# Attention in pairs of key blocks: full units of row maxima, VectorE's order written out, division two steps late, clearing spread out

## The chip, the cores and the metric

The kernel runs on one core of one Trainium2 chip. The metric is the device time of one execution in microseconds (us); lower is better. The engines are named as in the profile: PE (TensorE, matmuls), PEld (its weight loads), DVE (VectorE), ACT (ScalarE), POOL (GpSimd) and SP (SyncE, which here only issues DMAs).

## The reference, cut to what matters

The input x is 2 x 1024 tokens of 512 numbers, in float32. Four residual layers follow one another, each on the layer-normed x: causal attention with 16 heads of 32, a mixture of 32 experts of which each token takes the 8 with the largest router logits, a state-space layer (in chunks of 64), and a gated feed-forward whose weights are looked up in a table of 16 numbers. The change lies in the attention and in the routing that is interleaved with it:

```python
x = x + attn(_layernorm(x))
x = x + experts(_layernorm(x))      # router: top 8 of 32, softmax over them
x = x + ssd(_layernorm(x))
x = x + ghost_ffn(_layernorm(x))

def attn(x):
    q = einsum('btc,hcd->bhtd', x, Wq) + bq     # k, v likewise
    scores = einsum('bhtd,bhsd->bhts', q, k) * scale
    probs = softmax(scores + causal)
    y = einsum('bhts,bhsd->bhtd', probs, v)
    return y.reshape(B, T, H * D) @ Wo + bo
```

## The kernel before, in words

Attention (`_attention`) works on groups of four heads of one batch: four groups per batch, so eight groups, 0 to 7. The 1024 tokens of a batch are eight blocks of 128. A group's queries come as two halves (qt 0 and 1) of 512; with the causal mask the first half sees key blocks 0 to 3 and the second 0 to 7, so a group has twelve steps (qt, kb), and `group` (L660) loops over them.

The softmax is made in two passes. The row maxima come first and from a matmul of their own. `maxima` (L432) computes, for each query block tb and each pair pr of heads, the scores of that block against its keys in pieces of at most 512 keys, two heads (hh) at a time in two PSUM tiles `sp`; VectorE reduces them into `mx`: `junk` (L462) masks and reduces the diagonal 128 keys, and a `tensor_reduce` (L468) the rest. A piece of one (tb, pr) is one unit, so there are 8 x 2 units for the first 512 keys and 4 x 2 for the others: 24 steps of the generator's loop per group, many of them with fewer than four blocks of keys. `fold` (L473) turns the maxima of half a group, negated, with a transposing matmul (`nm_ps`) and ACT copies (L487) them into extra rows of q, so that the second pass subtracts them within its matmul.

The second pass has `scores` (L524) and `values` (L554). `scores` makes four matmuls `st` (one per head) for one step; ACT takes their exp into `pT` (L544), and POOL clears the triangle of a diagonal block (L547). `values` multiplies `pT` with v, where 32 columns of ones beside the values make the row sums, into two PSUM tiles `y`. After the last key block of a half, `finish` (L496) divides: ACT copies `y` to `raw`, four DMAs write the sums to DRAM, one DMA reads them back spread over 128 partitions (`sm`), VectorE takes the reciprocal (L509), one DMA writes it (`inv`), four DMAs broadcast it (`rb`), and four multiplications on VectorE give `yT` (L519). `finish` stands, whole, at the place where the half ends.

The groups are pipelined: while group i runs its twelve steps, `maxima(i + 1)` is interleaved, and at its end `project_qk(i + 2)` (L401: four `pq` of four matmuls; VectorE adds the bias for q, L423, ACT for k, L427), with the last `values` after the first `pq`. Beside a group something else may run, one generator step at a time: `normalise(1)` (layer norm of the second batch, from group 1 on) and `route_first` (L585: routing of the first batch's eight blocks in four pairs, and after each pair its 16 sends, in groups 4 on). Group 4 also holds `project_v` of the second batch. `project_out(0)` stands between groups 3 and 4, and `route_last` with `project_out(1)` after group 7.

A send (`_Router.send`, L253) is an indirect DMA on POOL that writes 128 token rows to their slots in `rows`, in DRAM. The slots must have been cleared: `clear` (L334) has 178 DMAs on SP's queue, 160 of 272.5 KB into `rows` and 18 of 256 KB into the accumulators. Four are issued at each step of a group, without a wait on anything of the group, and SP's queue is the one that the DMAs of `finish`, the weights and the routing use too. The sends wait for the clears of `rows` (the list `ready`). The routed rows (`row`, written at L162) lie in a pool of three buffers, of which `blank`, the source of the clears, holds one; the rows of a later pair take a buffer again only when the sends that read it are done.

PSUM has eight banks: two of tag "f" (maxima, projections, nm_ps, routing), four of tag "s" (`st`) and two for `y`. PE's order is the program's order, because the attention is built inside `manual_schedule(engines={PE})`; the order of VectorE, ACT, POOL and SP is left to the scheduler. Whatever an engine's instruction waits for, what is queued behind it on that engine waits too.

Of the kernel before, what the change touches and what calls it, by code (L numbers as in the profile page):

```python
# [18 lines left out]
P = 128  # L19
# [82 lines left out]
class _Router:  # L102
# [7 lines left out]
    def __init__(self, tc, g, x_sb, xnT, a, pool, rows, acc, left, ready):  # L110
        nc = tc.nc
        self.tc, self.g, self.x_sb, self.xnT = tc, g, x_sb, xnT
        self.pool, self.rows, self.acc, self.left, self.ready = pool, rows, acc, left, ready
        self.sent = [[[] for _ in range(TOPK)] for _ in range(B)]
        self.earlier = None
        self.over = pool.tile([P, 1], I32, tag="over", name="over")
        self.wr = pool.tile([P, NCC, E], F32, tag="wr", name="wr")
        nc.scalar.dma_start(out=self.wr, in_=a["wr"])
        self.ones = pool.tile([P, P], F32, tag="ones", name="ones")
        nc.gpsimd.memset(self.ones, 1.0)  # L120
        self.before = pool.tile([P, P], F32, tag="before", name="before")
        nc.gpsimd.affine_select(
            self.before, self.ones, pattern=[[1, P]], compare_op=ALU.is_gt, fill=0.0, base=0,
            channel_multiplier=-1,
        )
        self.number = pool.tile([P, NBLK], I32, tag="number", name="number")
        nc.gpsimd.iota(self.number, pattern=[[P, NBLK]], base=0, channel_multiplier=1)
        self.spare = pool.tile([P, NBLK, TOPK], I32, tag="spare", name="spare")
        nc.gpsimd.iota(
            self.spare, pattern=[[P * TOPK, NBLK], [P, TOPK]], base=1 + E * CAP,  # L130
            channel_multiplier=1,
        )
        self.first = pool.tile([P, E], I32, tag="first", name="first")
        nc.gpsimd.iota(self.first, pattern=[[CAP, E]], base=1, channel_multiplier=0)
# [10 lines left out]
    def route(self, blocks, wk, row_of, bank):  # L145

        tc, g, x_sb, xnT = self.tc, self.g, self.x_sb, self.xnT
# [20 lines left out]
        for i, blk in enumerate(blocks):  # L168
            pt = bank("t", [P, NCC, P])
            for cc in range(NCC):  # L170
                nc.tensor.transpose(
                    pt[:, cc, :], xr[i][:, cc * P : (cc + 1) * P], g["ident"]
                )
            nc.scalar.copy(xnT[:, :, blk * P : (blk + 1) * P], pt)
            yield
        pl = bank("l", [P, n, E])
        for i, blk in enumerate(blocks):
            for cc in range(NCC):
                nc.tensor.matmul(
                    pl[:, i, :], lhsT=xnT[:, cc, blk * P : (blk + 1) * P],  # L180
                    rhs=self.wr[:, cc, :], start=cc == 0, stop=cc == NCC - 1,
                )
# [65 lines left out]
    def send(self, routed, places):  # L248
        tc = self.tc
        blocks, xr, idx = routed  # L250
        for k in places:
# [12 lines left out]
            yield  # L264
# [16 lines left out]
def _attention(tc, g, x_sb, xnT, a, router):  # L281
# [8 lines left out]
    with ExitStack() as ctx:  # L290
# [6 lines left out]
        rp = inner.enter_context(tc.tile_pool(name="at_row", bufs=3))  # L297
# [36 lines left out]
        def clear():  # L334
            for n in range(E * CAPB):
                ready.append(
                    nc.sync.dma_start(out=rows[1 + n * P : 1 + (n + 1) * P, :], in_=blank)
                )
                yield
            for n in range(NBLK + 1):  # L340
                nc.sync.dma_start(out=acc[1][n * P : (n + 1) * P, :], in_=blank[:, :D])
                yield
            nc.sync.dma_start(out=acc[0][NT : NT + P, :], in_=blank[:, :D])
            yield

        clearing = clear()


# [3 lines left out]

        v = kv.tile([P, TBLK, H // 2, 3, DH], F32, tag="v", name="v")
# [9 lines left out]
        def normalise(b):  # L363

            for grp in range(TBLK // 4):
# [4 lines left out]
                for i, blk in enumerate(blocks):  # L370
# [3 lines left out]
                    before = xn, blk  # L374
# [7 lines left out]
        def project_v(b):  # L382
            for sb in range(TBLK):
                pv = ps_f.tile([P, D], F32, tag="f", name="pv")
                for cc in range(NCC):
                    nc.tensor.matmul(
                        pv,
                        lhsT=xnT[:, cc, b * T + sb * P : b * T + (sb + 1) * P],
# [12 lines left out]
        def project_qk(i):  # L401
# [4 lines left out]
            for hf in range(2):  # L406
                tok = slice(hf * 512, (hf + 1) * 512)
                for s, (dst, wn) in enumerate(((q, "wq"), (k, "wk"))):
                    pq = ps_f.tile([P, 512], F32, tag="f", name="pq")
                    for cc in range(NCC):  # L410
# [3 lines left out]
                            rhs=xnT[:, cc, b * T + hf * 512 : b * T + (hf + 1) * 512],  # L414
# [16 lines left out]

        def maxima(i, psum, tag):  # L432
# [3 lines left out]
                [P, TBLK, 2, 2, 3], F32, tag="mx", name="mx", bufs=2  # L436
            )
            nc.gpsimd.memset(mx, F32_MIN)
            for tb in range(TBLK):
                n = (tb + 1) * P  # L440
                for pr in range(2):
                    for ci, k0 in enumerate(range(0, n, 512)):
                        k1 = min(n, k0 + 512)
                        sp = [
                            psum.tile([P, 512], F32, tag=tag, name="sp") for _ in range(2)
                        ]
                        for hh in range(2):
                            rows = slice(hh * 64, hh * 64 + 64)
                            nc.tensor.matmul(  # L449
                                sp[hh][:, : k1 - k0],  # L450
                                lhsT=q[rows, pr, tb * P : (tb + 1) * P],
                                rhs=k[rows, pr, k0:k1],
                                start=True,
                                stop=True,
                            )
                        for hh in range(2):
                            m = mx[:, tb, pr, hh]
                            rest = k1 - k0
                            if k1 == n:
                                rest -= P  # L460
                                junk = wk.tile([P, P], F32, tag="junk", name="junk", bufs=1)
                                nc.vector.tensor_tensor_reduce(  # L462
                                    out=junk, in0=sp[hh][:, rest : rest + P], in1=cmask,
                                    scale=1.0, scalar=F32_MIN, op0=ALU.add, op1=ALU.max,
                                    accum_out=m[:, 2:3],
                                )
                            if rest:
                                nc.vector.tensor_reduce(  # L468
                                    m[:, ci : ci + 1], sp[hh][:, :rest], AX.X, ALU.max
                                )  # L470
                        yield
# [23 lines left out]

        def finish(i, qt, y):  # L496

# [10 lines left out]
            nc.sync.dma_start(out=sm, in_=sums.rearrange("j (c f) -> (j c) f", f=16))  # L508
            nc.vector.reciprocal(sm, sm)  # L509
            nc.sync.dma_start(out=inv.rearrange("j (c f) -> (j c) f", f=16), in_=sm)  # L510
            rb = wk.tile([P, 2, 512], F32, tag="rb", name="rb", bufs=1)
            for j in range(4):
# [3 lines left out]
                )  # L516
            for j in range(4):
# [6 lines left out]
        def scores(i, qt, kb):  # L524
# [5 lines left out]
            for j in range(4):  # L530
# [9 lines left out]
                pT = router.pool.tile(  # L540
                    [P, ROW], F32, tag=f"row{turn[0] % TBLK}", name="pT"
                )[:, :512]
                turn[0] += 1
                nc.scalar.activation(pT[:, c0:], st[:, c0:], AF.Exp)  # L544
# [7 lines left out]
            return ps  # L552

        def values(i, qt, kb, ps, y):  # L554
# [11 lines left out]
            if kb == 4 * qt + 3:  # L566
                finish(i, qt, y)
# [17 lines left out]
        def route_first():  # L585

            def bank(tag, shape):
# [5 lines left out]
            for blk in range(0, TBLK, 2):  # L593
                routed = yield from router.route([blk, blk + 1], wk, row_of, bank)
                yield from router.send(routed, range(TOPK))
# [43 lines left out]
        def first_groups():  # L639
# [12 lines left out]
            for u, _ in enumerate(maxima(0, ps_s, "s")):  # L652
                if u % 2:
                    next(other)
                if u == 11:
# [4 lines left out]
        def group(i, beside):  # L660
# [7 lines left out]
            pending = y = None  # L668
            blocks = [(qt, kb) for qt in range(2) for kb in range(4 * qt + 4)]
            for n, (qt, kb) in enumerate(blocks):  # L670
                if kb == 0:
                    y = [ps_y.tile([P, 512], F32, tag="y", name="y") for _ in range(2)]
                ps = scores(i, qt, kb)
                next(more, None)
                for _ in range(4):
                    next(clearing, None)
                next(beside, None)
                if n == 1 and gi == 0 and b:
                    run(project_v(b))
                    load_w("wo", "wvo")  # L680
                if pending is not None:
                    values(*pending)
                pending = (i, qt, kb, ps, y)
                next(more, None)
                next(beside, None)
                if n == 5 and follows:
                    fold(i + 1, 0)
            ahead = project_qk(i + 2) if i + 2 < ngr else iter(())
            next(ahead, None)
            values(*pending)  # L690
            run(ahead)
            if follows:
# [3 lines left out]
        with tc.manual_schedule(engines={mybir.EngineType.PE}):  # L696
            first_groups()
            fold(0, 1)
            beside = iter(())
            for i in range(ngr):  # L700
                if i == 1:
                    beside = normalise(1)
                group(i, beside)
                if i == NG - 1:
                    run(beside)
                    run(project_out(0, yT[0]))
                    load_w("wv", "wvo")
                    beside = route_first()
            run(beside)
        y = yT[0]  # L710
# [224 lines left out]
def _left_over(tc, g, x_sb, xnT, a, left, acc):  # L935
# [3 lines left out]
    with ExitStack() as ctx:  # L939
# [5 lines left out]
        dr = ctx.enter_context(tc.tile_pool(name="ex_dr", bufs=1, space=DRAM))  # L945

        wT = dr.tile([E, NT], F32, tag="wT", name="wT")
# [465 lines left out]
def kernel(ctx: ExitStack, tc: tile.TileContext, a: dict, out: bass.AP):  # L1413
# [26 lines left out]
    with tc.tile_pool(name="tokens", bufs=1, side="right") as tok:  # L1440
        x_sb = tok.tile([P, NBLK, D], F32, tag="x", name="x_sb")
        xnT = tok.tile([P, NCC, NT], F32, tag="xnT", name="xnT")
        router = _Router(tc, g, x_sb, xnT, a, pool, rows, acc, left, [])
        _attention(tc, g, x_sb, xnT, a, router)
# [4 lines left out]
        with tc.If(some > 0):  # L1449
            _left_over(tc, g, x_sb, xnT, a, left, acc[0])  # L1450
# [130 lines left out]
```

## Time and profile before

| what | us |
| --- | --- |
| median of three runs | 3076.01 (3062.91 to 3078.62) |
| the profiled execution | 3071.58 |
| its span on the profile | 3069.7 |
| PE busy, of the span | 2794.5 (91%) |
| DVE busy | 1381.8 (45%) |
| ACT busy | 915.5 (30%) |
| POOL busy | 617.9 (20%) |
| mean clock granted to PE | 0.951 |
| norms, first projections, maxima of group 0 (12.8 to 104.3) | 91.5 |
| the eight groups with project_out(0) (104.8 to 852.5) | 747.7 |
| after attention, up to the experts' first matmul (to 976.5) | 124.0 |
| experts and the second layer (to the end) | 2093.2 |

The profile is of one execution. Busy time is the time in which an engine executes something; [...] The granted clock is 1.00 at full speed. A row of waits reads "engine, what it waited to do, what it waited for: us in total, times, longest". A row of a timeline reads "start, duration, engine, line, operation, how many in one stretch", and in brackets the idle time before it and what ended that.

### The profile page before, as it was taken

Reading aid. Unit: us, or ns where it says so; the run is one execution under the profiler, and the core shown is the slowest. Engines: PE = TensorE matmul, PEld = TensorE weight load, DVE = VectorE, ACT = ScalarE, POOL = GpSimd, SP = SyncE. Lnnn points to the kernel's source line nnn. Section 1 sums busy time; section 2 is a strip of 40 time slices with the busy share of each in tenths; the row PEclk is TensorE's granted clock in tenths of the full one; section 3 lists DMA queues with packets and bytes.
Section 4 is the critical chain, followed back from the end, with each engine's and each line's share of the span. In section 5 each row is a group of like instructions: output and inputs, shape, how many; then the busy total and the mean of one; then the engine's idle time right before and its main releaser. Section 6 shows DMA issues by size and latency. Waiting matters only on the chain. (4 is left out here: it accounts for less than half of the span.)

```text
span 3069.7 us, 34003 instructions
## 1 busy us (share of the span) xinstructions
PE 2794.5 (91%) x11848; PEld 1612.2 (53%) x11848; DVE 1381.8 (45%) x3803; ACT 915.5 (30%) x1863; POOL 617.9 (20%) x786
## 2 busy tenths in 40 slices
PE   7789999778972999999999969999999997999999
PEld 3334444333352555555555548777777774444444
DVE  6434443433431999999311034445554554101010
ACT  1323332232411333333333333444444432110010
POOL 4012110433135333333333311011110111000000
PEclk9979999988976999999999989999999998999999
DMA  9950001221047988787788630111111113000000
GB/s 312 284 175 8 7 6 59 93 96 63 12 136 283 282 190 193 190 194 180 169 181 178 111 87 15 43 29 43 44 41 36 29 51 139 0 0 31 10 18 24
DMA packets 237682, 310.29 MB, mean 101 GB/s; under 512 B 60000, under 2 KB 126560, under 8 KB 236480
## 3 DMA queue, kind: packets, MB, share of 16 engines
q1 hardware_dynamic: 202928, 229.53, 24.6%
q0 software_dynamic: 33280, 77.68, 12.8%
q8 instruction: 97, 1.59, 0.2%
q10 hardware_dynamic: 1296, 0.83, 0.1%
q14 instruction: 81, 0.66, 0.1%
HBM read 159.12 MB, written 148.85 MB: 100 GB/s over the span
## 5 line engine op out<-in xcount | busy, mean ns | idle before, releaser
L841 PE MATMUL pg<-xgT,wgu 128*128 128x320 f32 x1536 | 467.8, 449 | 0.5 <-ACT xgT L833 0.5
L885 POOL DMA_INDIRECT acc<-y,tok x160 | 270.9, 1693 | 534.0 <-ACT y L884 409.5
L841 PEld LDWEIGHTS pg<-xgT,wgu 128*128 128x128 f32 x1536 | 283.8, 195 | 169.5 <-issue 56.7
L745 DVE SCALAR_TENSOR_TENSOR acc<-hit,lut,acc 128x688 f32<-128x688 bf16 (+2 forms) x405 | 345.2, 855 | 5.3
L449 PE MATMUL sp<-ka,qa 64*128 64x512 f32 (+3 forms) x768 | 214.0, 538 | 65.6 <-DVE mx L468 33.4
L1134 PE MATMUL pf<-xT,win 128*128 128x256 f32 x1024 | 242.5, 385 | 4.9 <-ACT gate L1162 4.1
L544 ACT ACTIVATE pT<-st 128x512 f32<-128x512 f32 (+3 forms) x384 | 159.2, 496 | 238.8 <-PE st L533 218.5
L1134 PEld LDWEIGHTS pf<-xT,win 128*128 128x128 f32 x1024 | 187.0, 190 | 38.2 <-PE pf L1134 6.0
L468 DVE TENSOR_REDUCE mx<-sp 128x1 f32<-128x512 f32 (+3 forms) x320 | 164.3, 527 | 76.5 <-PE sp L449 68.9
L449 PEld LDWEIGHTS sp<-ka,qa 64*128 64x128 f32 x768 | 93.2, 197 | 174.5 <-issue 55.8
L547 POOL TENSOR_SCALAR_AFFINE_SELECT pT<-pT 128x128 f32<-128x128 f32 x256 | 72.9, 297 | 505.3 <-ACT pT L544 500.6
L533 PE MATMUL st<-qa,ka 64*128 64x512 f32 (+3 forms) x768 | 168.4, 534 | 1.3 <-ACT pT L544 1.3
L832 PE MATMUL xg_ps<-ident,xg 128*128 128x128 f32 x640 | 99.1, 280 | 67.3 <-issue 67.3
L1394 PE MATMUL pg<-xT,wg 128*128 128x512 f32 (+1 forms) x352 | 158.6, 593 | 0.1
L1394 PE MATMUL pu<-xT,wu 128*128 128x512 f32 (+1 forms) x352 | 158.2, 592 | 0.0
L1403 DVE TENSOR_TENSOR hT<-s,pu 128x512 f32<-128x512 f32 (+1 forms) x44 | 30.2, 687 | 281.0 <-PE pu L1394 281.0
L871 PE MATMUL po<-wd,hT 128*128 128x512 f32 x320 | 153.7, 594 | 1.8 <-ACT y L884 1.8
L1376 PE MATMUL po<-wd,hT 128*128 128x512 f32 (+1 forms) x352 | 152.6, 592 | 0.0
L559 PE MATMUL y<-pT,v 128*64 128x512 f32 (+3 forms) x768 | 150.7, 514 | 0.0
L884 ACT ACTIVATE y<-po,rw 128x512 f32<-128x512 f32 x160 | 104.1, 685 | 156.0 <-PE po L878 151.5
L462 DVE CUSTOM_DVE_ANT_0 junk<-sp,cmask 128x128 f32<-128x128 f32 x256 | 73.8, 288 | 160.5 <-PE sp L449 146.0
L253 POOL DMA_INDIRECT rows<-row,idx x128 | 124.5, 973 | 103.5 <-issue 80.0
(185 smaller groups left out, 3832.7 us busy)
## 6 DMA issues: line engine op xcount, KB each, us to landing
rows<-blank SPq DMA_DIRECT2D x160, 272.5 KB
xg<-rows SPq DMA_DIRECT2D x32, 1362.5 KB
csb<-cs_rows SPq DMA_DIRECT2D x128, 128.0 KB
wgu<-in_wg_dram SPq DMA_DIRECT2D x32, 256.0 KB
wgu<-in_wu_dram SPq DMA_DIRECT2D x32, 256.0 KB
wd<-in_wd_dram SPq DMA_DIRECT2D x32, 256.0 KB
wd<-in_wd_dram SPq DMA_DIRECT2D x64, 128.0 KB
x<-x SPq DMA_DIRECT2D x32, 256.0 KB
```

What stands on the lines that cost most here:

```text
L449: nc.tensor.matmul(sp[hh][:, : k1 - k0], lhsT=q[rows, pr, tb * P : (tb + 1) * P], rhs=k[rows, pr, k0:k1], start=True, stop=True,)
L468: nc.vector.tensor_reduce(m[:, ci : ci + 1], sp[hh][:, :rest], AX.X, ALU.max)
L533: nc.tensor.matmul(st[:, c0:], lhsT=k[half, j // 2, kb * P : (kb + 1) * P], rhs=q[half, j // 2, qt * 512 + c0 : (qt + 1) * 512], start=Tru ...
L544: nc.scalar.activation(pT[:, c0:], st[:, c0:], AF.Exp)
L559: nc.tensor.matmul(y[j // 2][half, c0:], lhsT=v[:, kb, h // 2, h % 2 : h % 2 + 2, :].rearrange("p k d -> p (k d)"), rhs=ps[j][:, c0:], sta ...
L745: nc.vector.scalar_tensor_tensor(acc, hit, lut[:n, k : k + 1], acc, ALU.mult, ALU.add)
L841: nc.tensor.matmul(pg, lhsT=wgu[:, cc, m * P : (m + 1) * P], rhs=xgT[:, cc, cols], start=cc == 0, stop=cc == NCC - 1,)
L871: nc.tensor.matmul(o, lhsT=hT[:, j * P : (j + 1) * P], rhs=wd[:, 0, :], start=True, stop=False,)
L885: nc.gpsimd.indirect_dma_start(out=acc[turn[0] % 2][:, :], out_offset=bass.IndirectOffsetOnAxis(ap=tok[:, j : j + 1], axis=0), in_=y, in_o ...
L1134: nc.tensor.matmul(pf, lhsT=w[wn][:, cc, c0 : c0 + P], rhs=xT[st][:, cc], start=cc == 0, stop=cc == NCC - 1,)
L1376: nc.tensor.matmul(po, lhsT=hT[:n, fc, j * P : (j + 1) * P], rhs=wd[:n, fc, :], start=fc == 0, stop=fc == NFC - 1,)
L1394: nc.tensor.matmul(dst[:n, :], lhsT=w[:, cc, fc * P : fc * P + n], rhs=xT[:, cc, :], start=cc == 0, stop=cc == NCC - 1,)
```

## The change

It changes the order of the work in attention, and some buffers; the arithmetic per element stays.

- **Maxima.** The pieces of (tb, pr) are packed one after another into units of four key blocks (512 columns of a pair of `sp` tiles), so a unit may hold pieces of more than one query block and a piece may be cut. There are 18 full units, of 27 pieces in all. `mx` has four columns instead of three. Three units are made per pair of key blocks.
- **Order of a group.** The twelve steps go in six pairs. In a pair (n, n + 1) the order on PE is: a unit (A), scores of n, a unit (B), scores of n + 1, a unit (C), values of n - 1, values of n. At n = 4, where the second half begins, C comes after the values of n - 1. The work beside comes one step after C and one after the values of n, and then three sends. `fold(i + 1, 0)` comes at the end of n = 4. At the group's end: one `pq`, the values of step 11, the other three `pq`, and `fold(i + 1, 1)`.
- **VectorE** is added to `manual_schedule`: its order is now the program's order too.
- **Division.** `finish` becomes a generator of three parts: up to the read of `sm` at once; reciprocal, `inv` and `rb` at the next `tick`; the multiplications at the one after. `tick` stands once in each pair, after the values of n - 1 and before those of n, but for the pair at n = 4. In project_out(0) one tick stands before and one after its first four blocks.
- **Clearing.** Eight clears per pair of key blocks instead of four per step, and each waits for the last exp of that pair (`clear_some`).
- **Routing.** It has its own transposed tiles `rt_xT`; routing and sending are two generators, a send yields after every DMA, and the pool of rows has four buffers instead of three.
- **Other moves.** `normalise(1)` goes from group 1 to group 2, and what is left of it is run at that group's end. `xnT` covers one batch instead of two. `pT` rotates over twelve buffers (eight of the router's, four new ones). `_left_over`, in a branch for tokens beyond an expert's capacity, makes its own `xnT`. The maxima of group 0 have 18 steps in `first_groups` too.

The diff, cut to its core:

```diff
+        units = [[]]
+        room = 4
+        for tb in range(TBLK):
+            for pr in range(2):
+                k0 = 0
+                while k0 <= tb:
+                    if not room:
+                        units.append([])
+                        room = 4
+                    k1 = min(tb + 1, k0 + room)
+                    units[-1].append((tb, pr, k0, k1))
+                    room -= k1 - k0
+                    k0 = k1
```
```diff
+        def clear_some(n, after):
+
+            for dst, src in islice(clearing, n):
+                t = nc.sync.dma_start(out=dst, in_=src)
+                _after(tc, t, after)
+                if src is blank:
+                    ready.append(t)
```
```diff
+        def tick():
+
+            if later and next(later[0], later) is later:
+                later.pop(0)
...
             nc.sync.dma_start(out=sm, in_=sums.rearrange("j (c f) -> (j c) f", f=16))
+            yield
             nc.vector.reciprocal(sm, sm)
...
+            yield
             for j in range(4):
                 r = (0, 96)[j % 2]
                 nc.vector.tensor_tensor(
...
             if kb == 4 * qt + 3:
-                finish(i, qt, y)
+                later.append(finish(i, qt, y))
+                next(later[-1])
```
```diff
-            for n, (qt, kb) in enumerate(blocks):
...
+            for n in range(0, len(blocks), 2):
                 next(more, None)
-                for _ in range(4):
-                    next(clearing, None)
+                for m in (n, n + 1):
+                    ps, e = scores(i, *blocks[m])
+                    made.append(ps)
+                    if m == n:
+                        next(more, None)
+                clear_some(8, e)
+                turning = n and blocks[n][1] == 0
+                if not turning:
+                    next(more, None)
                 next(beside, None)
...
+                if n:
+                    one(n - 1)
+                if turning:
+                    next(more, None)
+                else:
+                    tick()
+                one(n)
                 next(beside, None)
-                if n == 5 and follows:
+                for _ in range(3):
+                    next(sending, None)
+                if n == 4 and follows:
                     fold(i + 1, 0)
```
```diff
-        with tc.manual_schedule(engines={mybir.EngineType.PE}):
+        with tc.manual_schedule(engines={mybir.EngineType.PE, mybir.EngineType.DVE}):
```

## The prediction

> **What bounds the kernel now.** I read the page's busy shares and its 40 slices first (one slice is 3069.7/40 = 76.7 us), then a table of the stages with each engine's busy time and granted clock, then the waits of the first 900 us, and last the timelines inside the stages that came out long.
>
> ```profile
> span 3069.7 us, 34003 instructions
> ...
> PE 7789999778972999999999969999999997999999
> ...
> PEclk9979999988976999999999989999999998999999
> DMA  9950001221047988787788630111111113000000
> ```
>
> TensorE (PE) is the bound nearly everywhere. The change touches only slices 2 to 12: attention runs from 104.8 us (first st of group 0) to 852.5 us (last y). PE is weak there in slices 2 (7), 7 to 9 (9, 7, 7) and 10 (8); DMA is at 9 only in slices 1 and 2. The chain that ended last on the page starts at about 2396 us and says nothing of attention, so stages are compared. The rows run from the first st of one group to that of the next; the fifth row is project_out of batch 0, the last what follows attention, up to the experts' first matmul. Columns: us, then busy us of PE, PEld, DVE, ACT, POOL, granted clock, DMA share, GB/s.
>
> ```profile
> 104.80:215.90 111.10, 82.87 (x331) 37.75 (x330) 37.09 (x121) 32.40 (x65) 14.15 (x36) 0.85 0.79 239
> 215.90:304.90 89.00, 80.71 (x361) 37.14 (x360) 42.06 (x129) 36.02 (x73) 19.18 (x41) 0.94 0.03 7
> 304.90:383.00 78.10, 72.78 (x331) 33.52 (x330) 39.46 (x124) 31.21 (x65) 12.84 (x35) 1.00 0.04 8
> 383.00:464.50 81.50, 73.91 (x330) 34.33 (x329) 41.06 (x127) 33.72 (x69) 13.10 (x37) 0.98 0.04 10
> 464.50:492.10 27.60, 27.60 (x64) 12.03 (x64) 13.84 (x29) 4.11 (x6) 0.00 (x0) 1.00 0.15 57
> 492.10:631.30 139.20, 110.02 (x457) 52.52 (x456) 53.27 (x188) 36.58 (x72) 44.68 (x71) 0.93 0.25 87
> 631.30:741.50 110.20, 96.45 (x395) 46.14 (x394) 46.41 (x177) 31.66 (x66) 41.23 (x64) 0.84 0.21 75
> 741.50:815.40 73.90, 61.40 (x297) 29.21 (x296) 33.23 (x115) 28.73 (x60) 12.51 (x36) 0.91 0.09 25
> 815.40:852.50 37.10, 36.29 (x194) 14.57 (x193) 5.98 (x10) 22.86 (x53) 9.93 (x37) 1.00 0.06 16
> 852.50:976.50 124.00, 52.52 (x203) 36.01 (x202) 30.05 (x121) 10.83 (x19) 62.08 (x69) 0.63 0.62 209
> ```
>
> Group 2 is the yardstick: nothing beside it, clock 1.00, 78.1 us of which PE is idle 5.3. Against it groups 0, 4, 5 and 6 are long by idle PE (28.2, 29.2, 13.8, 12.5 us) and by a low clock. The waits name what VectorE (DVE) stood behind:
>
> ```profile
> DVE sm L509 <- DMA sm<-sums: 34.2, 3, 21.2
> PE sp L449 <- DVE mx L468: 33.4, 19, 16.7
> DVE yT L519 <- DMA rb<-inv: 32.9, 15, 5.3
> DVE row L162 <- DMA rows<-row,idx: 19.9, 3, 10.7
> PE nm_ps L485 <- DVE qa L423: 8.1, 1, 8.1
> ```
>
> So in group 0 the reciprocal (L509) waits 21.2 us for sums that lie behind the clearing DMAs, a reduce of the maxima waits behind it in DVE's queue, and PE behind that: one hole of 16.70 us, as the timeline of PE and then of DVE shows.
>
> ```profile
> 157.99 1.38 PE L449 MATMUL sp<-ka,qa 64*128 64x256 f32 x3 [16.70 <-DVE mx L468]
> ```
> ```profile
> 157.13 0.25 DVE L509 RECIPROCAL sm<-sm 128x16 f32<-128x16 f32 x1 [21.21 <-DMA sm<-sums]
> 157.30 1.22 DVE L468 TENSOR_REDUCE mx<-sp 128x1 f32<-128x512 f32 x2
> ```
>
> In groups 4 and 5 the same queue stands behind row (L162), which waits for a row buffer that unfinished sends still read.
>
> **The change, part by part.** The sums are of this execution (3071.6 us; span 3069.7 and 1.9 around it), 4.4 below the median of 3076.0.
>
> *Division two steps late, clearing spread, DVE ordered (group 0).* The stalls that go: PE idle 16.70 + 3.21 + 4.54 (at 141.3, 162.8 and 193.5 us) = 24.4, and the half clock that follows them: of 158.0-162.2, 165.6-172.4 and 196.3-203.2 us some 15.6 us are busy, so about 7.8 lost. What is late next: with no clears the division's first half took 3.7 us in group 2 (raw at 328.35, reciprocal at 332.07), the second 3.8 (to 335.89). SP's queue issued 67 of the 160 large clears in 62.33 us (its timeline from 20.87 us), 0.93 us each, so the 8 issued per pair of key blocks are 7.4 us ahead of sums or of inv and rb, which share that queue; and the clears now wait for the pair's last exp, with those DMAs behind them. First half at worst 3.7 + 7.4 = 11.1 us, against a pair of steps of 78/6 = 13 us: it just fits, with 2 us to spare. 178 clears at 48 per group end in group 3; they leave the stage before attention, whose PE (84.8 busy of 91.5 us) has little to gain from that. Group 0: 78.5 (below) + 1.5 = 80, from 111.1: **-31**.
>
> *A quiet group.* 24 pieces of maxima become 27 in 18 full units. PE: 3 pieces at 0.12 us, +0.4. DVE: 24.9 to 27.4 us per group from the rows 0.216 (junk), 0.227-0.604 (reduce); DVE is busy 39.5 of 78.1, so this hides unless it falls in a chain. Gone: the 0.36-0.95 us gaps between the small 128-wide pairs at each group's start (3.3 us) and some of the stretch of later pairs: -3.6 together. New: at a group's start A goes before S, and both its banks wait for ACT (ka 2.75, then nm copies 2.02): PE idle 4.4 us instead of 3.0 (+1.4), and the fold at n = 4 holds a bank ahead of A (+2.2). Sum +0.4: **78.5**, against 78.1. Bounds: all waits gone, 73; every wait doubled, 84.
>
> [...] At 218.7 us the trace has a gap of 1.60 us and then clock 0.50 for 220.2-230.5; at 307.7 a gap of 1.61 and clock 1.00; after 3.21 us (162.8) half clock for 6.8 us. [...] before already pays 4.8 (group 1) and 1.6 (387.5 us) at such places. I take **+8**; bounds 0 and +18.
>
> *normalise(1) from group 1 to 2.* 10.9 us over the quiet group before (7.9 PE, 3.0 idle; part of it half clock). Groups 1 + 2 were 167.1. Now 79.5 + 89.5 = 169: **+2**, as DVE in program order makes later maxima wait for the norms and ACT's square root with its table load (1.28). Its 8 POOL adds move too; POOL is idle four fifths.
>
> *Group 3 and project_out(0).* 109.1 to 78.5 + 29.5 = 108: **-1**; the last mult now lies between blocks 4 and 5 of it.
>
> *Routing in groups 4 to 6.* Sends go one to a step, three steps a pair, apart from routing, and row buffers go from three to four. POOL is charged 1.27 us a send (0.96 + 0.30), 64 sends as before. Pair 3's rows wait for pair 1's sends, which lie some 40 us earlier, so the stalls on L162 (8.73, 8.11, and 2.53 with it) should go. Routing needs 8.7 us of PE per group at full clock (23.7 over quiet in group 5, of which 15 is half clock in 36 us) plus 6 of DVE answers that PE sees. Group 4: 78.5 + 27.6 (project_v) + 15 = 121 from 139.2, **-18**. Group 5: 78.5 + 15 = 93.5 from 110.2, **-17**. Group 6: 66.5 from 73.9, **-7**: its 7.46 us hole (ACT ka L427, released by "remote" while POOL sends) is the least certain.
>
> *Group 7* has no maxima; S S V V in a row needs eight st from four banks, each freed by an exp of 0.52: 40.5 from 37.1, **+3**. pT with twelve buffers, router's own xT and a half-size xnT cost nothing: the same copies by the same engines; without that cover the copies are below 1 us each. _left_over is in a branch not taken.
>
> *After attention* the 64 sends of the second batch (81 us on POOL, 895.7 to 976.6) set the experts' start as before; all shifts.
>
> Sum: -31 + 2 - 1 - 18 - 17 - 7 + 3 = -69, with +8 for the clock **-61**: 3010.6 in the profiled execution, **3015** beside the median.
>
> **The rivals.**
> - *Larger gain.* Ordered DVE and full units also take half of the 10.8 us that each quiet group loses against its bare PE work (67.3), in seven groups: 7 x 5.4 = 38 more, about 2977. For it: 33.4 us of PE waiting for mx. Against: each piece costs DVE more, and the start of a group gets worse.
> - *Small gain.* In-order DVE waits on ACT (norms, key step of routing, 3-4 us a pair over four pairs) and "remote" waits stay: groups 4 to 6 gain 15 instead of 42, about 3042; with a point of ticks too, 3056.
> - *Nothing happens.* The holes come from DMA and POOL, and only move: within 15 us of 3076.
> - *Slower.* Ticks stand in DVE's fixed order. If the sums or rb land later than the tick in groups 0 to 3 (178/48 = 3.7 groups, 4 ticks each, 15 ticks), DVE and then PE wait X us each: 15X. It eats the 61 at X = 4.1 and is slower beyond measurement from X = 5.1: at X = 6, 3105. For it: margin of 2 us, and clears that wait for exps hold the queue. Against: 8 clears drain within a pair.
>
> **How the numbers follow.** Chances: forecast (-40 to -80) 0.45, larger gain 0.24, small gain 0.17, nothing 0.08, slower 0.06. What this kernel's measurement can tell from no change is about 0.5%, 15 us. Faster 0.86, same 0.08, slower 0.06. The range 2974 to 3056 runs from the larger gain to the small one.
>
> **What would show it.** Right: group 0 near 80 us, no sm wait over 5 us, DMA share near 0.6 spread over groups 0 to 3; no PE hole over 5 us in groups 4 and 5; quiet groups 77 to 80; a 4.4 us gap at each start, with the clock at half behind it. Wrong: waits of DVE on sm or yT by DMA in groups 0 to 3, group 5 still over 100, a quiet group below 75 or above 82, or the experts' start set by something other than the sends.

## The result, and the profile after

The changed kernel takes 3046.8 us (median of six runs, 3038.3 to 3050.3) against 3078.8 us for the kernel before (median of six, 3062.9 to 3084.1): a ratio of 0.9896 (95% interval 0.9870 to 0.9922), 32 us less. The forecast was 61 less. The profiled execution took 3045.5 us, span 3043.3. Its slices (page, part 2; one is 76.1 us):

```profile
span 3043.3 us, 34138 instructions
...
PE   7988999887954999999999969999999997999999
...
PEclk9998999898967999999999989999999998999999
DMA  2365431132058988787878631111111123000000
```

DMA, at 9 in the first two slices before, is now spread over slices 1 to 6. PE's weak slice 2 became a 9, but slices 8 to 10 are 8, 8, 7. The stages follow, with the columns of the prediction's table; a group here begins with the end of the previous fold, as its first st no longer comes first:

```profile
106.60:185.90 79.30, 72.90 (x337) 36.83 (x336) 36.28 (x121) 32.50 (x65) 13.24 (x35) 0.96 0.61 174
185.90:268.90 83.00, 74.35 (x337) 37.02 (x336) 39.24 (x126) 31.70 (x65) 12.81 (x35) 0.96 0.58 169
268.90:361.00 92.10, 82.69 (x369) 44.30 (x368) 50.25 (x152) 42.12 (x79) 23.55 (x44) 0.91 0.51 153
361.00:447.00 86.00, 75.89 (x338) 37.81 (x337) 39.15 (x127) 33.98 (x69) 12.81 (x35) 0.94 0.36 115
447.00:477.40 30.40, 29.46 (x65) 12.68 (x65) 7.46 (x11) 1.96 (x2) 0.00 (x0) 0.95 0.16 60
477.40:600.50 123.10, 112.96 (x455) 57.70 (x454) 53.34 (x178) 36.41 (x70) 28.99 (x55) 0.94 0.17 61
600.50:706.40 105.90, 87.09 (x381) 45.69 (x380) 51.67 (x184) 39.96 (x76) 45.07 (x69) 0.90 0.25 91
706.40:790.40 84.00, 67.92 (x333) 36.70 (x332) 37.49 (x144) 29.21 (x62) 24.72 (x48) 0.88 0.17 61
```

Group 0 went from 111.1 to 79.3 us, as forecast: its reciprocal, which had stood for 21.21 us, now waits 1.28.

```profile
149.24 0.25 DVE L545 RECIPROCAL sm<-sm 128x16 f32<-128x16 f32 x1 [1.28 <-DMA sm<-sums]
```

Everywhere else the rows are longer than forecast, and none has the clock at 1.00, as group 2 had before.

Since single executions differ, both kernels were profiled once more, on one other chip (`c1` and `c2` below). All lengths in the next table are taken at the same events: from the first transpose of a group's last fold (nm_ps) to the next, project_out(0) by its own matmuls, the tail from the last y to the experts' first gate matmul.

| stage | before | after | before, again | after, again | forecast |
| --- | --- | --- | --- | --- | --- |
| start to group 0 | 91.5 | 93.2 | 89.3 | 93.5 | as before |
| group 0 | 111.1 | 79.4 | 104.2 | 77.6 | 80 |
| group 1 | 89.0 | 83.0 | 86.2 | 80.8 | 79.5 |
| group 2 | 78.1 | 92.1 | 78.1 | 89.6 | 89.5 |
| group 3 with project_out(0) | 109.7 | 117.0 | 112.9 | 112.4 | 108 |
| group 4 | 138.1 | 122.5 | 139.4 | 115.8 | 121 |
| group 5 | 110.7 | 105.9 | 100.8 | 100.9 | 93.5 |
| group 6 | 73.9 | 84.0 | 65.9 | 72.4 | 66.5 |
| group 7 | 37.7 | 41.7 | 37.7 | 41.7 | 40.5 |
| tail | 126.7 | 121.3 | 127.3 | 121.0 | as before |

So up to the experts the change saves 26.4 us in the first pair of executions and 36.1 in the second. (As whole executions c1 and c2 took 3054.7 and 3004.6 us; the other 14 us lie behind the experts' start, and c1 is 11 us above the median of before on its chip.) Three rows have the same sign and a like size in both: groups 0 and 4 save 31.7 + 15.6 or 26.7 + 23.6 us, and group 6 costs 10.1 or 6.4. What is known of why groups 5 and 6 are longer in the first pair than in the second, in both kernels, comes at the end of the experiments.

### The profile page after: what moved, and what is told of

Its sections match the earlier page's. It is cut to its first block, busy times and chain, and to the rows that moved or that the text cites. A ratio compares the mean times of both kernels' runs of the same rounds, so it can differ in the third digit from the quotient of the medians.

```text
span 3043.3 us, 34138 instructions
## 1 busy us (share of the span) xinstructions
PE 2790.3 (92%) x11912; PEld 1636.5 (54%) x11912; DVE 1382.7 (45%) x3819; ACT 927.9 (30%) x1871; POOL 618.8 (20%) x786
## 5 line engine op out<-in xcount | busy, mean ns | idle before, releaser
L474 PE MATMUL sp<-ka,qa 64*128 64x512 f32 (+3 forms) x832 | 234.4, 523 | 57.8 <-DVE mx L495 33.0
L570 PE MATMUL st<-qa,ka 64*128 64x512 f32 (+3 forms) x768 | 199.8, 549 | 1.4 <-ACT pT L583 1.3
L495 DVE TENSOR_REDUCE mx<-sp 128x1 f32<-128x128 f32 (+3 forms) x336 | 165.7, 509 | 59.1 <-PE sp L474 36.0
L474 PEld LDWEIGHTS sp<-ka,qa 64*128 64x128 f32 x832 | 106.6, 206 | 141.2 <-issue 55.0
L598 PE MATMUL y<-pT,v 128*64 128x512 f32 (+3 forms) x768 | 141.5, 503 | 9.9 <-POOL pT L586 6.1
```

The source lines that it names most:

```text
L474: nc.tensor.matmul(sp[hh][:, c0:c1], lhsT=q[half, pr, tb * P : (tb + 1) * P], rhs=k[half, pr, k0 * P : k1 * P], start=True, stop=True,)
L495: nc.vector.tensor_reduce(m[:, n : n + 1], sp[hh][:, c0:c1], AX.X, ALU.max)
L570: nc.tensor.matmul(st[:, c0:], lhsT=k[half, j // 2, kb * P : (kb + 1) * P], rhs=q[half, j // 2, qt * 512 + c0 : (qt + 1) * 512], start=Tru ...
L598: nc.tensor.matmul(y[j // 2][half, c0:], lhsT=v[:, kb, h // 2, h % 2 : h % 2 + 2, :].rearrange("p k d -> p (k d)"), rhs=ps[j][:, c0:], sta ...
```

## The experiments

They ran on three chips, each beside the kernel before on the same chip: e1 to e4 on chip 1 (median of before 3042.3 us), c1, c2, e5 and e7 on chip 3 (3043.5), e8 to e11 on chip 2 (3062.0). A ratio is to the kernel before on that chip.

**Two parts alone (e1).** The kernel before with `finish` in three parts, clears that wait, and ticks at every second step:

```diff
-                for _ in range(4):
-                    next(clearing, None)
+                clear_some(4, e)
...
+                if n % 2 == 0 and n != 4:
+                    tick()
```

> The kernel before with two parts of the change alone: the clears wait for the exp of their step (4 a step), and the division's reciprocal and multiplications come at ticks two and four steps later. VectorE keeps the scheduler's order, maxima their 24 units, routing and normalise their places. Theory (the hole of group 0 is the reciprocal standing ahead of maxima while its sums lie behind clears): group 0 falls from 111.1 to 80-84 us, groups 4 to 6 stay at 323 together, the whole is 25 to 33 us below before, so about what the full change gives. Rival (the order of VectorE is what frees group 0): the scheduler still puts a waiting reciprocal or multiplication ahead of maxima, group 0 stays above 95, and the whole gains 15 us or less.

Measured: 3032.3 us against 3042.3 of before on the same chip, 0.9952 (0.9931 to 0.9974): 10 us less by the medians, 15 by the ratio. Group 0 took 84.4 us, so theory holds for it: spread clears and late division carry most of group 0 without VectorE's order. What is missing against the full change (c2 below) lies mostly in group 4, 136.9 against 115.8 us: there VectorE still waits 11.8 and 10.6 us at L162.

**VectorE's order left to the scheduler (e5)**, with the two kernels once more.

```diff
-        with tc.manual_schedule(engines={mybir.EngineType.PE, mybir.EngineType.DVE}):
+        with tc.manual_schedule(engines={mybir.EngineType.PE}):
```

> The kernel before, unchanged, profiled beside the other runs of this call. Theory: stages as in its first profile for groups 0 to 3 (111, 89, 78, 82 us), but without the waits of VectorE and ACT that the trace can't name groups 5 and 6 come to about 99 and 66 us (as in the run with two parts alone), against 110.7 and 73.9. Rival: 110 and 74 again, and the change of the division and the clearing is what shortened them.

> The changed kernel, unchanged, profiled and timed beside the kernel before. Theory: the nameless waits were that execution's; groups 4 to 6 come to 115 + 101 + 73 = 289 us instead of 312, groups 1 and 3 stay at 81 to 83 and 84 to 86 us with the wait for rb, the ratio is 0.990 again. Rival (those waits belong to the sends): groups 4 to 6 again above 305.

> The changed kernel with VectorE's order left to the scheduler. Theory (late division and spread clearing carry group 0, VectorE's fixed order adds little): within 6 us of the changed kernel, and groups 0 to 3 within 2 us each. Rival (the fixed order is what keeps the maxima moving): a stale estimate puts a multiplication or a reciprocal ahead of maxima, PE holes of over 5 us appear, and it is over 15 us slower than the changed kernel.

Measured: c1 gave the stages above (groups 5 and 6: 100.8 and 65.9); c2 a ratio of 0.9885 (0.9861 to 0.9908), groups 4 to 6 together 289.0 us; e5 0.9963 (0.9949 to 0.9976), so 26 us slower than c2 on the same chip by the medians. My theory fell here: the fixed order is no extra. Taken away from the full change, it costs most of the 35 us. Without it the holes come back, PE first and VectorE after it:

```profile
647.70 1.09 PE L172 MATMUL rt_t<-ident,row 128*128 128x128 f32 x4 [11.53 <-DVE mx L495]
```
```profile
645.18 0.55 DVE L162 TENSOR_SCALAR row<-x_sb,ln_mv,ln_rs 128x512 f32<-128x512 f32 x1 [11.90 <-DMA rows<-row,idx]
```

The scheduler puts `row`, whose buffer is not free for another 11.9 us, ahead of a reduce that PE needs at once; in the program's order `row` comes later and its buffer is free. The same happens with a multiplication in group 0 (6.32 us for rb, PE 6.20). The prediction credited the end of the L162 stalls to the fourth row buffer and the sends' own generator; both are in e5 too, and the stall stays. It is VectorE's order that ends it: neither profile of the changed kernel has a wait at L162. In e5 one such stall is in group 4 (9.80 us, PE 9.37) and one has moved to group 5, so the two groups have to be read together: 240.2 us in c1, 234.7 in e5, 216.7 in c2.

**VectorE's order alone (e10)**, in the kernel before, with the division whole and the clears ahead.

> The kernel before with one part of the change alone: VectorE in program order too; the division stands whole where a half ends, the clears go ahead. Theory (fixed order only helps once the division's steps come late): each of the sixteen divisions holds VectorE for at least the 3.7 + 3.8 us of its two DMA round trips, less when PE has banks to go on with, so 3 to 6 us of PE for each: 50 to 100 us slower than before, more in group 0. Rival (the fixed order itself is the gain): 10 us or more faster than before.

Measured: 3156.9 against 3062.0 us, 1.0308 (1.0270 to 1.0347), 95 us slower. PE, then VectorE, in group 0:

```profile
164.41 2.52 PE L449 MATMUL sp<-ka,qa 64*128 64x512 f32 x4 [28.95 <-DVE mx L462]
```
```profile
154.77 0.25 DVE L509 RECIPROCAL sm<-sm 128x16 f32<-128x16 f32 x1 [21.57 <-DMA sm<-sums]
...
161.19 2.83 DVE L519 TENSOR_TENSOR yT<-raw,rb 32x512 f32<-32x512 f32 x4 [6.17 <-DMA rb<-inv]
```

In a fixed order both round trips, 21.57 and 6.17 us, lie bare on PE's path. So order alone costs 95 us, late division with spread clears alone gains 15, and with the rest they gain 35: the order pays only where nothing in it waits long.

**Clears that do not wait (e11).**

```diff
                 t = nc.sync.dma_start(out=dst, in_=src)
-                _after(tc, t, after)
```

> The changed kernel with clears that do not wait for an exp, so that SP issues them as early as its order lets it. Theory (spreading is needed beside the late division): the sums of group 0 lie some 20 us behind clears again, the tick after 13 us does not cover that, VectorE stops at the reciprocal in its fixed order, group 0 comes to 88-100 us instead of 77.6, groups 1 and 3 lose their waits for rb (77-80 us each), the whole between 3 us faster and 15 us slower than the changed kernel. Rival (two steps of lateness alone are enough): group 0 below 80 us and the whole 5 us or more faster.

Measured: 0.9981 (0.9967 to 0.9996). The same chip ran the kernel with clears last (below) at 0.9934, so this is about 14 us slower than that. Group 0 took 96.8 us, groups 1 and 3 77.0 and 81.1. The theory holds; VectorE's row is

```profile
166.27 0.25 DVE L544 RECIPROCAL sm<-sm 128x16 f32<-128x16 f32 x1 [15.55 <-DMA sm<-sums]
```

and PE lost 10.86 us behind it. Two steps of lateness do not cover a queue of clears; one needs the spreading too.

**Clears last in the pair (e2).**

```diff
-                clear_some(8, e)
...
                 next(beside, None)
+                clear_some(8, e)
```

> The changed kernel with the eight clears of a pair issued at the end of the pair, behind the DMAs of the tick and of the division, instead of ahead of them. Theory (inv and rb stand behind eight clears in SP's queue, VectorE waits 3.5 us for rb with its multiplications in fixed order, and PE loses 2.8 us and a half-clock window behind that): VectorE's waits for rb in groups 1 and 3 fall from 3.5 us to below 1, PE's holes of 2.8 and 3.0 us go, groups 1 and 3 come to about 79 and 82 us from 83.0 and 86.6, groups 0 to 3 together lose 9 to 13 us. Rival (the 2.8 us of multiplications ahead of the next maxima cost this wherever rb lands): the holes stay, the whole within 3 us of the changed kernel.

Measured: 3006.3 us, 0.9877 (0.9857 to 0.9896); by ratio 2 us better than c2, on another chip and within the intervals. By stage, against c2: group 1 77.6 from 80.8, group 3 80.0 from 83.4, group 0 78.1 from 77.6; from the start of group 0 to the last y 685.4 against 691.1. So the mechanism is there and smaller than I expected: groups 0 to 3, without project_out(0), are 6.7 us shorter than in c2, not 9 to 13. In the changed kernel SP issues inv behind eight clears and rb 5 us after inv; VectorE, SP and PE in group 1 (timelines, after):

```profile
199.92 0.24 DVE L545 RECIPROCAL sm<-sm 128x16 f32<-128x16 f32 x1
...
202.87 0.68 SPq L546 DMA_DIRECT2D inv<-sm  x1
208.11 1.71 SPq L550 DMA_DIRECT2D rb<-inv  x4
...
210.23 2.83 DVE L556 TENSOR_TENSOR yT<-raw,rb 32x512 f32<-32x512 f32 x4 [3.51 <-DMA rb<-inv]
...
213.91 2.32 PE L474 MATMUL sp<-ka,qa 64*128 64x256 f32 x7 [2.83 <-DVE mx L495]
```

From the reciprocal to rb it took 10.3 us, and VectorE stood ready for the multiplications after 6.8. The clock was 0.50 from 214.5 to 217.9 us, behind PE's hole of 2.83. With clears last, the wait splits and shrinks, and no hole of PE above 0.8 us is left in group 1 behind its start:

```profile
209.00 1.39 DVE L556 TENSOR_TENSOR yT<-raw,rb 32x512 f32<-32x512 f32 x2 [0.71 <-DMA rb<-inv]
210.56 1.40 DVE L556 TENSOR_TENSOR yT<-raw,rb 32x512 f32<-32x512 f32 x2 [0.16 <-DMA rb<-inv]
```

**Scores first at a group's start (e3).**

```diff
-                next(more, None)
+                if n:
+                    next(more, None)
                 for m in (n, n + 1):
                     ps, e = scores(i, *blocks[m])
...
                     if m == n:
+                        if n == 0:
+                            next(more, None)
                         next(more, None)
```

> The changed kernel with the first scores of each group ahead of its first unit of maxima, as before. Theory (PE idles 2.2 + 1.6 us at each start because the unit needs banks that ACT still reads, and the clock falls to half behind it): the start's idle time falls to 2 us or less, the half-clock window behind most starts goes, 2 to 3 us for each of seven groups, 12 to 20 us in all. Rival (both banks are freed at the same time anyway; the unit and with it VectorE only come 2 us later and the idle time moves to the next unit): within 4 us of the changed kernel, and half-clock windows at most starts remain.

Measured: 0.9891 (0.9873 to 0.9910), 695.9 us for the eight groups against 691.1 of c2. Theory fell, the rival holds: the 2.18 us hole went, the 1.61 us one stayed, and a new one of 1.1 to 1.6 us before the next unit appeared ("<-DVE mx"), since VectorE started later. The order at the start gains nothing by itself.

**Halves of the evictions to VectorE (e9, beside e8).**

```diff
+                        elif hf and j >= 2:
+                            nc.vector.tensor_scalar(o, pq[r : r + DH], bias, None, ALU.add)
...
+                copy = nc.vector.tensor_copy if hf and r > DH else nc.scalar.copy
```

> The changed kernel with the clears at the end of the pair (as in the run with clears last) and the sends eight at a time in the pairs n = 4 and 6, which have no diagonal selects, instead of three in every pair. Theory (in group 5 the diagonal selects stand behind sends in POOL's queue, PE waits 4.8 us for them at y and a half-clock window follows): that hole goes, group 5 falls from 101 to 94-96 us, the whole 4 to 7 us below the run with clears last (ratio to before about 0.985). Rival (the row buffers then come free later, and VectorE in fixed order stops at row): group 5 or 6 gets a hole at row of over 3 us and the whole is not faster than with clears last.

> The kernel of the run with sends placed, and at each group's end VectorE takes half of the last ka eviction and one of the two nm copies, with the maximum for fold taken before them. Theory (a group start idles 2.2 + 1.6 us because ACT does 2.75 us of ka and 2.0 us of nm alone): the idle time of a start falls from 3.8 to about 1.6 us and with it some half-clock windows, 2 to 4 us for each of seven starts, 15 to 25 us in all (ratio to before about 0.978). Rival (the first unit then waits for something else, or VectorE's added 2.5 us comes back later in the group): within 5 us of the run with sends placed.

Measured: e8 3038.8 us, 0.9934 (0.9911 to 0.9957); e9 3029.5 us, 0.9898 (0.9864 to 0.9932), on the same chip. The edit of e8 did nothing: POOL's order is the scheduler's, and the instructions of all five engines stand as in the run with clears last. So e8 tells nothing of sends; it is that program on another chip, which is used below. The same holds for the change itself: it writes three sends a pair, but in its profile the 64 sends still run in four bursts of 16, each 20 to 23 us long (the first from 540.9 to 561.1 us). e9 is 9 us better by median than e8 (the intervals overlap), and its groups from 0 to the last y take 704.4 instead of 713.6 us. The start of group 1 in the changed kernel, and in e9, where VectorE's row follows:

```profile
188.16 0.48 PE L474 MATMUL sp<-ka,qa 64*128 64x128 f32 x2 [2.18 <-ACT ka L437]
190.25 1.73 PE L474 MATMUL sp<-ka,qa 64*128 64x128 f32 x10 [1.60 <-issue]
```
```profile
190.15 0.76 PE L476 MATMUL sp<-ka,qa 64*128 64x128 f32 x2 [2.67 <-DVE ka L437]
191.41 2.04 PE L476 MATMUL sp<-ka,qa 64*128 64x128 f32 x10 [0.50 <-DVE qa L524]
```
```profile
188.49 1.52 DVE L437 TENSOR_SCALAR ka<-pq,bqk 32x512 f32<-32x512 f32 x2 [1.81 <-ACT ka L439]
```

The idle time falls from 3.8 us (3.5 in e8) to 3.2, not to 1.6. VectorE's half of ka began only when ACT's half had ended, so the first hole grew to 2.67 us; only the nm copies ran side by side, and only the second hole shrank. Why the halves of ka ran one after the other is open. Groups 0, 1 and 3 are 1.3 to 1.7 us shorter than in e8. That fits the theory that the eviction bounds a start, at half its size or less; with overlapping intervals the rival is not excluded.

**The old units (e7).**

> The changed kernel with the 24 units of before, four a pair (the fourth between the two values), instead of 18 full units, three a pair. Theory (full units take bank turns away: PE's own work in a quiet group was 72.8 us with 24 units and 70.9 with 18): quiet groups 2 to 4 us longer, the whole 12 to 25 us slower than the changed kernel. Rival (only the bytes count, and 24 pieces cost VectorE 2.5 us less per group): within 5 us, or faster.

Measured: 0.9922 (0.9894 to 0.9950), by median 10 us slower than c2 (the intervals overlap a little); the eight groups took 698.6 against 691.1 us. PE's own work (busy time less half of what fell at half clock; in the first profile of before, eight matmuls y<-pT,v of 128x512 took 1.94 us at clock 1.00, at 139.35 us, and 3.67 at 0.50, at 226.95) in groups 1 and 3 was 73.7 and 74.4 us against 71.0 and 71.7. So full units save 2.7 us of PE's work in such a group, but only about 1 us a group of the time: from group 0 to 6, e7 lost 21 us to half clock and c2 lost 30, which gave back much of it. The quiet group of before, with the same 24 units, had 72.8.

**No sends (e4).**

> The changed kernel without the 64 sends of the first batch (its tokens do not reach the experts; routing is still computed). Only groups 4 to 6 are read. Theory (bursts of sends on POOL hold up ACT, VectorE and the diagonal selects): groups 4 to 6 fall from 312.4 us together to about 285, the waits of VectorE and ACT that the trace can't name go, and so does the 6.1 us hole before y. Rival (routing's chain in VectorE's fixed order is what costs): 305 us or more.

Measured, in a single execution: groups 4 to 6 took 115.8 + 92.8 + 73.2 = 281.8 us. Against 312.4 of the first profile that looks like the theory; but c2 has 289.0 with the sends. So in these groups the sends cost 7 us, all of it in group 5 (8 us), where PE waits for selects that stand behind sends in POOL's queue (changed kernel, waits):

```profile
PE y L598 <- POOL pT L586: 6.1, 1, 6.1
```

In the changed kernel that hole ends at 686.85 us, and the clock was 0.50 from 685.5 to 692.4. In c2 the wait is 4.7. The other 23 us are those of the next paragraph.

**The waits without a name.** In the first profile of the changed kernel VectorE and ACT stand for 2 to 9 us at places that the trace puts down to "remote", all of them during a burst of sends on POOL, in groups 4 to 6, or ending within 3 us of its end:

```profile
DVE junk L488 <- remote: 14.6, 3, 7.2
...
DVE mx L495 <- remote: 12.2, 3, 6.3
...
ACT qa L514 <- remote: 9.4, 1, 9.4
```

The kernel before has them too (6.1, 13.0 and 11.2 us, in groups 5 and 6). In c2 and e2 there is none; in e8 there are

```profile
DVE mx L495 <- remote: 15.3, 3, 8.3
...
ACT qa L514 <- remote: 9.4, 1, 9.4
...
DVE junk L488 <- remote: 9.2, 2, 7.1
```

Since e8 is e2's program, groups 4 to 6 at 313.8 instead of 288.4 us are the price: 25 us. All four profiles from chip 2 have such waits and none of the eight from chips 1 and 3 has; for the first pair the chip is not on record. In the kernel before, groups 4 to 6 took 322.7 us with them and 306.1 without. What these waits are stays open: the run without sends was on a chip that does not show them, so it can't tell whether the sends cause them.

## Why the prediction was right, and where its sum was off

The direction, the mechanism of group 0 and the range held. The gain was about half of the sum: at 32 us it lies outside the band held likeliest (40 to 80) and fits the small-gain rival, which had groups 4 to 6 at 15 us (measured 10.3, in the second pair 17.1) and the whole near 3042. Of the signs of being wrong, four showed: VectorE waited on yT in groups 0 to 3, group 5 stayed over 100 us, a quiet group was above 82 (83.0; 80.8 in the second pair), and the experts' start no longer followed the last send. So the range was right for group 0's reason, and wide enough for the misses elsewhere. Term by term (first pair of profiles, the second in brackets):

- **Group 0, -31:** -31.7 (-26.7). Right. e1 has most of it without VectorE's order, e11 shows that lateness without spreading is not enough, and e10 that order alone is not. Spreading without lateness was not tried.
- **Quiet group, 78.5:** 83.0 (80.8) in group 1. The unit's cost had the wrong sign: three more pieces were to cost 0.4 us of PE, and full units saved about 1.8 against before (2.7 against e7). The step that was mis-sized is the place of the multiplications. The sum gave each half of the division a pair of 13 us, which is an average. The first half had that (12.2 us in group 0). The second took 10.3 us in group 1, no more than 3.8 + 7.4, but its place on VectorE came 6.8 us after the reciprocal (6.8 to 10.0 in groups 0 to 3, but for the last half, across project_out(0)). So rb came 3.5 us late (2.6), and PE lost 2.8 us (1.9). That is the "slower" rival at a small size: one tick in group 1 that cost PE more than a microsecond, not four, and e2 takes it away (77.6). The 67.3 us of bare PE work a group in the larger-gain rival have no working; PE's own work in such groups was 72.7 us before and 70.9 after.
- **The clock, +8 net:** the sum took 7.8 us of half clock out of group 0 and 15 out of group 5 and put 8 in. By the records, groups 0 to 6 with project_out(0) lost 38.6 us to half clock (half of PE's busy time in it) before and 42.9 after (30.9 and 30.5): nothing net, where about -15 had been taken. In the first pair groups 0 and 5 lost 6.8 and 7.8 us less, and groups 2, 3, 4 and 6 lost more than that again.
- **normalise, +2 for groups 1 and 2:** +8.0 (+6.1). Group 2 itself was 89.6 in the second profile, forecast 89.5; PE waits 3.5 us in it for a reduce behind the norms.
- **Group 4, -18:** -15.6 (-23.6). Right in size; but with the row buffers and without VectorE's order (e5), groups 4 and 5 together gain 5.5 us of the 23.5 in c2, so the order is the larger cause.
- **Group 5, -17, and group 6, -7:** -4.7 and +10.1 (+0.1 and +6.4). This is the largest miss, by 29 us (30). The sum took the length of group 5 in one execution, 110.7 us, as stalls that the change removes. The long PE holes behind L162 lie in group 4, not here; and in the other execution group 5 was 100.8 us, 7.8 of the difference being half clock. The sum left no half clock in group 5 but a share of the +8; 9.0 us stayed (8.4), and PE's idle time rose from 13.8 to 18.8 us (11.7 to 15.1): selects behind sends (6.1), a reduce behind the division's multiplications (2.4). Sends three to a pair, which the sum counted on, did not come about. And with two steps beside a pair instead of four, the routing of the last pair of blocks moves into group 6: PE's work there rose from 58.0 to 60.8 us, its idle time from 12.5 to 16.1, its half clock by 3.6.
- **Group 7, +3:** +4.1 (+4.1).
- **Start and tail, nothing:** +1.7 and -5.4 (+4.3 and -6.3). After the change the experts' first matmul no longer waits for the last send (952.9 against 954.7 us). The tail is 121 us in nearly every run built on the changed kernel and 126 to 127 in those built on the kernel before. Which edit does it was not tried.

The clock at the starts: after the change, half clock comes at all six starts at which units of maxima come first (groups 0 to 3, 5 and 6), for 3.4 us in group 1 and 6.8 in each of the others. Their holes are 2.0 to 2.2 us and then 1.3 to 1.6, not one of 4.4 as forecast. The length of the last hole alone does not tell in these traces whether the clock drops. Ahead of project_out(0), at the same place in both kernels, PE stood for 2.26 us before (to 464.45 us) and the clock stayed at 1.00; after the change it stood for 2.19 us (to 446.98), and the clock was 0.50 from 446.6 to 450.0. A hole of 1.94 us in the changed kernel's group 0 (to 164.62) kept 1.00 as well. What decides was not shown, and the +8 of the sum was the author's estimate.

The best version by its own chip's ratio is the changed kernel with clears last, 0.9877, which is not to be told from the change itself (0.9885 and 0.9896). With the shared evictions (0.9898, on the chip with the nameless waits, where clears last had 0.9934) it gains perhaps another 9 us (the intervals overlap); that was not run on a chip without those waits.

## What to carry to other kernels

A fixed order on an engine is worth what its longest wait allows: give every step that waits for a round trip a place later than the round trip takes, keep other DMAs of its queue behind it, and bound each leg of the trip by itself, against its own place in the order and not an average. Before a stall is booked as a gain, ask what the engine does next, and whether the stall is there in a second execution. A reordering edit on an engine whose order a scheduler makes may change nothing; compare the orders first.

## What was not expected of the hardware

The same program took 25 us more in groups 4 to 6 on one chip than on another, with waits of VectorE and ACT about POOL's indirect DMAs that the trace can't name (8.3 and 9.4 us the longest). And the kernel before ran at medians of 3042 to 3079 us from one group of runs to the next, 1.2%, more than the change gains: only ratios to the kernel before on the same chip say anything here.
